# Context sums kept in memory between two cross attentions, and squares taken in one operation

## The chip, the cores and the metric

The kernel runs on one core of a Trainium2 chip. The metric is device time in microseconds (us) of one execution; a time given for a kernel is the median of several runs. The profile is of one further execution, with its own time.

The engines by the names of the profile: PE is the matrix engine (PEld its weight loads, which overlap the matmuls), DVE is VectorE, ACT is ScalarE, POOL is GpSimd, and SP is SyncE, which here only issues DMAs. A "q" behind a name is the engine's own instruction queue. Each engine takes its instructions in the order of its queue.

## The reference

Two layers are applied to `x` (8 x 64 x 512, float32) with a context of 8 x 1601 x 512. Each layer is a cross attention to the context, a self attention (the first layer's works on the Fourier transform of x), and a feed-forward part (a mixture of experts in layer 0, ternary weights in layer 1). What matters here are the two cross attentions, which read the same context:

```python
x = x + _L0_xattn_ref(_layernorm(x), ctx_1024, mask, L0_xattn_Wq, L0_xattn_Wkv, ...)
...
x = x + _L1_xattn_ref(_layernorm(x), ctx_1024, ctx_1024, L1_xattn_Wq, ..., L1_xattn_Wk, ..., L1_xattn_Wv, ...)
```

The first has 16 heads of 64; the kernel folds its key weights into the queries, so that scores are products of the context itself with folded queries, and mixes the context's rows before it applies the value weights. The second has 16 heads of 32, and projects keys and values of all 1601 tokens. Its keys and queries are normalized within each head (mean taken off, divided by the root of the mean square), so that it needs the sum of squares over each head of every key.

## The kernel before

**Seven products instead of eight.** The large products of both cross attentions are done by a scheme of Strassen and Winograd: both factors are cut into four quarters, and seven products of quarters or of sums of quarters replace eight. For the left factor (the context) the sums are made by POOL in `Quarters.left`, four operations at lines 136 to 139 on a tile `q` with seven slots. Slots 0 to 3 hold the loaded quarters, slots 4, 5 and 6 three of the sums, and the fourth sum overwrites slot 2:

```python
nc.gpsimd.tensor_add(q[:, 4, :], q[:, 2, :], q[:, 3, :])
nc.gpsimd.tensor_sub(q[:, 5, :], q[:, 4, :], q[:, 0, :])
nc.gpsimd.tensor_sub(q[:, 2, :], q[:, 0, :], q[:, 2, :])
nc.gpsimd.tensor_sub(q[:, 6, :], q[:, 1, :], q[:, 5, :])
```

**The first cross attention** (`l0_xattn`, from the start to about 1460 us) goes in 17 steps, two for each of the 8 batches (one for each half of the heads) and one behind. The first 12 x 128 tokens of a batch's context are six pairs of 128-token tiles. In each step `load_columns` (L177) loads the transposed context of the six pairs, two DMAs of 256 KB each (L183), and makes their sums with POOL operations of 128x256; the scores (matmuls at L465) use them. `load_rows` (L191, DMAs at L197) does the same with the rows of the context for `attend` (matmuls at L582). Columns and rows take turns in one pool of six buffers, so that a row pair can be loaded when the scores have used the column pair in its buffer, and the next column pairs when `attend` has used the rows. The transposed context of a batch is loaded twice, once for each half. Folded queries come by L224, value weights by L573, and the last 65 tokens by L651 and L662. The tail is not part of the quarters.

**The second cross attention** (`l1_xattn`, about 1840 to 3020 us) loads the transposed context once for each batch, as three groups of 512 tokens. `load` (L1426) has two DMAs of 512 KB for 256 tokens each (L1430), then `Quarters.left` with operations of 128x512: a quarter is 256 tokens by half of the 512 features. `project_keys` and `project_values` run the seven products with matmuls at L1514, through `Sevenfold`. A product is copied from the accumulator by ACT (`keep`, L1485), or added to a kept one by DVE (`sum`: L1493 for keys, L1506 for values), or finished by ACT (`last`, L1497 and L1509). During the attention of batch b the program projects the values of b and the keys of b + 1, and as soon as group g has given its values, `load(b + 1, g)` refills its buffer. The scores are matmuls at L1689 and are scaled by DVE at L1701. The softmax has DVE folds over key tiles (L1709 to L1714, for the maximum and the sum), a subtraction (L1731), and ACT's Exp (L1732). The weighted sum of values is L1740.

When the keys of two column groups of 128 features are done, `finish` (L1789) calls `squares_of` and `deviations` for each of the two. `squares_of` (L1548) squares the 1601 keys in four ACT operations of 384, 384, 384 and 449 elements (L1552) into four buffers, `deviations` sums each piece over heads with one matmul (L1564), copies the sums (L1566, L1567), turns them (L1570), and POOL raises them to the power -1/2 (L1577).

At its start, the second attention projects the last 65 tokens of all batches and stores them in memory (keys L1606, values L1617, copied from the accumulators by ACT at L1605 and L1616).

**What sets the order.** The program text does not set the order of an engine's queue. A planner in the compiler goes through the program with its own model of times and puts an instruction into its engine's queue when the model finds it ready, earlier program lines first among those ready. It also sets all waits. SP's queue is made in the same way, and an instruction in it that waits holds up those behind it.

Of the kernel before, what the change touches and what calls it, by code (L numbers as in the profile page):

```python
# [10 lines left out]
F32 = mybir.dt.float32  # L11
# [3 lines left out]
AF = mybir.ActivationFunctionType  # L15
# [5 lines left out]
P = 128  # L21
B, S, D = 8, 64, 512
NT = B * S // P
DC = D // P
NKV = 1601
# [94 lines left out]
QH = HALF // 2  # L120
NPAIR = LAST // 2
# [17 lines left out]
        nc.gpsimd.tensor_sub(q[:, 6, :], q[:, 1, :], q[:, 5, :])  # L139


def l0_xattn(K, x, d, ternary):

# [5 lines left out]
    tc, nc = K.tc, K.nc  # L149
    with ExitStack() as es:  # L150
        wp = es.enter_context(tc.tile_pool(name="a_w", bufs=1))
        cp = es.enter_context(tc.tile_pool(name="a_ctx", bufs=NPAIR))
# [21 lines left out]
            pool, tag = ((ps_x, "x"), (ps_y, "y"), (ps_z, "z"), (ps_m, "mm"))[turn[0] % 4]  # L174
            return pool.tile(shape, F32, tag=tag, name=name)

        def load_columns(b):  # L177

            pairs = []
            for i in range(NPAIR):  # L180
                q = cp.tile([P, 7, QH], F32, tag="pair", name="ctxT")
                for j in range(2):
                    nc.sync.dma_start(  # L183
                        q[:, ds(2 * j, 2), :].rearrange("p h (c n) -> p (h c) n", n=P),
                        d["ctxT"][b, :, ts(2 * i + j, P)].rearrange("(c p) n -> p c n", p=P),
                    )
                Quarters.left(nc, q)
                pairs.append(q)
            return pairs

# [114 lines left out]
        m32 = wp.tile([B * NK, P], F32, tag="m32", name="m32")  # L305
        nc.scalar.dma_start(m8, d["mask"])
        load_tails(0)
        ctxT = load_columns(0)
        place = [tp.tile([P, 4, 3, QH], F32, tag="pt", name="stage").rearrange("p a b q -> p (a b q)") for _ in range(2)]
        qk = wp.tile([P, DC, HALF], F32, tag="qk", name="qk")  # L310
        qT = piece([NG, P], "qT")
# [333 lines left out]
        for step in range(2 * B + 1):  # L645
            if step < 2 * B:
                b, half = divmod(step, 2)
                if step:
                    now, ctxT = queries_of(b, half), load_columns(b)
                    if half == 0:  # L650
                        nc.sync.dma_start(  # L651
                            ctxT_tail[:, :, :TAIL], d["ctxT"][b, :, LAST * P :].rearrange("(c p) n -> p c n", p=P)
                        )
                s, m = scores(b, now, ctxT)
                top = top_of(m)
                if step == 1:
                    between = keys_side_of_rest(columns_of(norm_rest, NT - 1))
            if before:
                b0, half0 = divmod(step - 1, 2)
                attend(half0, *before, load_rows(b0), o[:, :, b0 % 2, :], step == 1)  # L660
                if half0 and b0 + 1 < B:
                    nc.sync.dma_start(ctx_tail[:TAIL], d["ctx"][b0 + 1, LAST * P :, :])  # L662
# [732 lines left out]
        self.fourth()  # L1395


def l1_xattn(K, x, d, ahead, queries_done, in_last):

# [6 lines left out]
    with ExitStack() as es:  # L1406
# [1 line left out]
        ep = es.enter_context(tc.tile_pool(name="d_e", bufs=1, reuse_waits="tile"))  # L1408
        cp = es.enter_context(tc.tile_pool(name="d_c", bufs=GROUPS, reuse_waits="tile"))
        wp = es.enter_context(tc.tile_pool(name="d_w", bufs=1, reuse_waits="tile"))  # L1410
        qp = es.enter_context(tc.tile_pool(name="d_sq", bufs=4, reuse_waits="tile"))
        rp = es.enter_context(tc.tile_pool(name="d_r", bufs=2, reuse_waits="tile"))
        ps_x = es.enter_context(tc.tile_pool(name="d_ps_x", bufs=2, space=PSUM, reuse_waits="tile"))
        ps_y = es.enter_context(tc.tile_pool(name="d_ps_y", bufs=2, space=PSUM, reuse_waits="tile"))
# [10 lines left out]

        def load(b, g):  # L1426

            q = cp.tile([P, 7, 2 * SET], F32, tag="ctxT", name="ctxT")
            for j in range(2):
                nc.sync.dma_start(  # L1430
                    q[:, ds(2 * j, 2), :].rearrange("p h (c n) -> p (h c) n", n=SET),
                    d["ctxT"][b, :, ds((2 * g + j) * SET, SET)].rearrange("(c p) n -> p c n", p=P),
                )
            Quarters.left(nc, q)
            return q

        def rights(w, name):
# [40 lines left out]
        class Keys:  # L1478
# [7 lines left out]

            def to(self, i, j):
                c = self.m + 2 * j
                return kT[c][:, ds((2 * self.g + i) * SET, SET)], bk[:, c : c + 1]

            def sum(self, i, j, ps, other):
                out, bias = self.to(i, j)
                nc.vector.scalar_tensor_tensor(out, ps, bias, other, ALU.add, ALU.add)  # L1493

            def last(self, i, j, ps):
                out, bias = self.to(i, j)
                nc.scalar.activation(out, ps, AF.Identity, bias=bias, scale=1.0)  # L1497

        class Values(Keys):


            def to(self, i, j):
                return v[:, 4 * self.g + 2 * i + self.m, ts(j, QH)]

            def sum(self, i, j, ps, other):
                nc.vector.tensor_add(self.to(i, j), ps, other)  # L1506
# [13 lines left out]
        def project_keys(q, g, m):  # L1520
            run.add(
                product(
                    lambda n, e: wk_of[n][:, e, ts(m, P)],
                    lambda n, e: q[:, Quarters.LEFT[n], ts(e, SET)],
                ),
                Keys(g, m),
            )

        def project_values(q, g, i):
            run.add(  # L1530
                product(
                    lambda n, e: q[:, Quarters.LEFT[n], ds(e * SET + i * P, P)],
                    lambda n, e: wv_of[n][:, e, :],
                ),
                Values(g, i),
            )
# [718 lines left out]
def program(tc, d):  # L2255
    nc = tc.nc
    with tc.tile_pool(name="const", bufs=1) as cp, tc.tile_pool(name="memory", bufs=1, space=DRAM) as memory:
# [5 lines left out]
        l0_xattn(K, x, d, w)  # L2263
# [26 lines left out]
        with tc.tile_pool(name="early", bufs=NT - 1) as sp:  # L2290

            def in_last():
                known.extend(K.statistics(sp, x[:, t : t + 1, :]) for t in range(NT - 1))

            l1_xattn(K, x, d, ahead, queries.close, in_last)
            keys.close()
            l1_tail(K, x, d, w, known)

# [93 lines left out]
```

## Time and profile before

| | |
|---|---|
| runs | 3199.24 us median of 3 (3198.28 to 3200.02) |
| profiled execution | 3206.62 us |
| its span, first to last instruction | 3204.8 us |
| mean granted clock of PE in it | 0.972 |
| POOL in `Quarters.left`, first attention, columns: 4 x 96 operations of 128x256 | 302.8 us |
| the same, rows | 296.6 us |
| POOL in `Quarters.left`, second attention: 4 x 24 operations of 128x512 | 146.8 us |
| POOL at L1577: 32 operations | 277.1 us |
| ACT at L1552: 96 operations of 384 (516 ns) and 32 of 449 (571 ns) | 67.8 us |
| DMA, mean over the span | 109 GB/s |

How to read the profile: a line of the timeline gives the start and the duration in us, the engine, the line of the kernel, the operation, what it writes and reads, shapes, and how many instructions are merged; in brackets stands how long the engine had been idle before it, and who ended that. A line of the waits gives who waited for whom, the time in total, how many times, and the longest. A line of the windows gives for a stretch of time its length and the busy time of PE, PEld, DVE, ACT and POOL (with instruction counts), then the mean granted clock of PE as a share of full speed, the share of the DMA engines' time in use, and GB/s.

### The profile page before, as it was taken

The page shows a single profiled execution, that of the slowest core. Times are in us where ns is not written, and L with a number is a line of the kernel's source. Part 1 is how long each engine was busy: PE and PEld are TensorE (multiplying, and loading weights), DVE is VectorE, ACT ScalarE, POOL GpSimd, SP SyncE. Part 2 cuts the span into 40 slices and gives each one's busy share as a digit, 9 for nine tenths or more (in the row PEclk, how much of TensorE's full clock was granted, in tenths as well). Part 3 has the DMA queues.
Part 4 walks back from the last instruction along what each step waited for, and adds up shares of the span by engine and source line. Part 5 has one row for each costly group of instructions (what it writes and reads, how often), then busy time and mean ns, then how long its engine had stood idle before and what let it go on. Part 6 is the DMA issues. An engine that isn't in the chain of part 4 may idle for free.

```text
span 3204.8 us, 42460 instructions
## 1 busy us (share of the span) xinstructions
PE 3080.4 (96%) x16347; PEld 2319.3 (72%) x16353; DVE 1895.4 (59%) x3168; ACT 855.8 (27%) x1716; POOL 1132.7 (35%) x1052
## 2 busy tenths in 40 slices
PE   8999999999999999999999999999999999999886
PEld 7777778888887788886544466777777777777653
DVE  4745555565566666665332346775756657576646
ACT  2222232222122322221122232323233232323223
POOL 5433325455444444441100053334253333424000
PEclk9999999999999999999999999989999999999788
DMA  7354554233434543226599632010101101010250
GB/s 215 92 166 145 157 177 121 89 109 106 138 92 142 186 139 99 89 85 221 181 350 340 220 95 86 7 41 9 56 17 31 45 17 41 26 35 3 102 83 14
DMA packets 341495, 349.88 MB, mean 109 GB/s; under 512 B 41102, under 2 KB 255126, under 8 KB 340142
## 3 DMA queue, kind: packets, MB, share of 16 engines
q1 hardware_dynamic: 335065, 329.84, 33.3%
q10 hardware_dynamic: 5589, 15.24, 1.3%
q8 instruction: 130, 2.13, 0.3%
q0 software_dynamic: 640, 2.10, 0.2%
q14 instruction: 71, 0.58, 0.1%
HBM read 315.07 MB, written 32.05 MB: 108 GB/s over the span
## 4 chain that ended last, share of the span: by engine, by line
PE 54%; DVE 8%; ACT 2%; issue 2%; DMA 1%; POOL 0%; SPq 0%; POOLq 0%; ACTq 0%; DVEq 0%
PE x_ps L1514 9%; PE y_ps L1514 7%; PE s_ps L1689 4%; PE acc L1740 4%; PE oe_ps L1228 3%; PE h_ps L1201 3%; PE x_ps L582 3%; PE x_ps L465 3%; PE sum_ps L1564 2%; PE z_ps L582 2%; PE z_ps L465 1%; DVE s L1701 1%; DVE s L1731 1%; PE y_ps L582 1%; ACT s L1732 1%
## 5 line engine op out<-in xcount | busy, mean ns | idle before, releaser
L1577 POOL TENSOR_TENSOR r<-r,minus_half 128x52 f32<-128x52 f32 x32 | 277.1, 8675 | 353.7 <-DVE r L1576 353.7
L136 POOL TENSOR_TENSOR ctxT<-ctxT 128x256 f32<-128x256 f32 (+1 forms) x120 | 112.3, 936 | 659.0 <-DMA ctxT<-in_ctxT 449.6
L465 PE MATMUL x_ps<-qt,ctxT 128*128 128x256 f32 x1152 | 285.9, 382 | 7.2 <-DVE s L430 4.0
L582 PE MATMUL x_ps<-pt,ctx 128*128 128x256 f32 x1152 | 280.4, 381 | 4.0 <-DVE a L558 3.1
L465 PEld LDWEIGHTS x_ps<-qt,ctxT 128*128 128x128 f32 x1152 | 216.2, 190 | 49.2 <-DVE s L430 9.2
L582 PEld LDWEIGHTS x_ps<-pt,ctx 128*128 128x128 f32 x1152 | 216.3, 189 | 38.0 <-DVE a L558 3.2
L1689 PEld LDWEIGHTS s_ps<-qb,kT 64*128 64x128 f32 x1664 | 175.7, 208 | 63.1 <-issue 29.2
L1689 PE MATMUL s_ps<-qb,kT 64*128 64x128 f32 x1664 | 208.4, 314 | 9.7 <-DVE s L1701 8.4
L446 DVE TENSOR_TENSOR m<-m,s 128x512 f32<-128x512 f32 x176 | 140.4, 798 | 92.2 <-ACT s L444 89.5
L136 POOL TENSOR_TENSOR ctx<-ctx 128x256 f32<-128x256 f32 x96 | 72.3, 753 | 340.1 <-DMA ctx<-in_ctx 286.2
L1701 DVE TENSOR_TENSOR s<-s_ps,r 128x512 f32<-128x512 f32 x192 | 126.3, 681 | 33.8 <-PE s_ps L1689 31.4
L1740 PEld LDWEIGHTS acc<-s,v 128*64 128x64 f32 x1664 | 99.5, 141 | 51.9 <-issue 42.3
L498 DVE TENSOR_TENSOR s<-s,top_ps 128x1024 f32<-128x1024 f32 (+1 forms) x112 | 123.2, 1136 | 21.6 <-PE top_ps L488 21.6
L1731 DVE TENSOR_TENSOR s<-s,top_ps 128x1664 f32<-128x1664 f32 x64 | 117.9, 1884 | 30.3 <-PE top_ps L1727 30.3
L430 DVE SCALAR_TENSOR_TENSOR s<-y_ps,bias,p 128x256 f32<-128x256 f32 x96 | 46.3, 483 | 143.9 <-PE y_ps L465 143.6
L1740 PE MATMUL acc<-s,v 128*64 128x128 f32 x1664 | 125.2, 286 | 5.7 <-ACT s L1732 5.7
L1732 ACT ACTIVATE s<-s 128x1664 f32<-128x1664 f32 x64 | 101.7, 1591 | 73.9 <-DVE s L1731 73.9
L499 ACT ACTIVATE s<-s 128x1024 f32<-128x1024 f32 (+1 forms) x112 | 110.8, 996 | 26.9 <-DVE s L498 22.6
L1514 PE MATMUL x_ps<-wv_of,ctxT 128*128 128x256 f32 x384 | 100.3, 395 | 18.3 <-DVE v L1506 18.3
L1201 PE MATMUL h_ps<-w,tok 128*128 128x512 f32 x256 | 117.3, 593 | 0.0
L1228 PE MATMUL oe_ps<-w,hT 128*128 128x512 f32 x256 | 115.6, 593 | 0.0
L139 POOL TENSOR_TENSOR ctxT<-ctxT 128x256 f32<-128x256 f32 (+1 forms) x120 | 115.6, 963 | 0.0
(471 smaller groups left out, 6542.3 us busy)
## 6 DMA issues: line engine op xcount, KB each, us to landing
w<-in_L0f_W SPq DMA_DIRECT2D x64, 1024.0 KB
ctxT<-in_ctxT SPq DMA_DIRECT2D x192, 256.0 KB
ctx<-in_ctx SPq DMA_DIRECT2D x192, 256.0 KB
ctxT<-in_ctxT SPq DMA_DIRECT2D x48, 512.0 KB
wvT<-in_L0x_WvT SPq DMA_DIRECT2D x16, 1024.0 KB
qk<-qk_all SPq DMA_DIRECT2D x15, 1024.0 KB
qk_all<-stage SPq DMA_DIRECT2D x32, 384.0 KB
wraw<-in_L1f_w1T SPq DMA_DIRECT2D x16, 512.0 KB
```

The costliest lines, as they stand in the source:

```text
L136: nc.gpsimd.tensor_add(q[:, 4, :], q[:, 2, :], q[:, 3, :])
L446: nc.vector.tensor_max(self.m, self.m if k else self.s[:, LAST, :], self.s[:, k, :])
L465: nc.tensor.matmul(ps, lhsT=ctxT[i][:, Quarters.LEFT[n], ts(e, P)], rhs=right[n][:, e, :], start=start and e == 0, stop=e == 1, skip_group ...
L582: nc.tensor.matmul(ps, lhsT=ctx[pair][:, Quarters.LEFT[n], ts(m, P)], rhs=right[n][:, i, :], start=start and i == 0, stop=i == 2, skip_gro ...
L1201: nc.tensor.matmul(ps, lhsT=self.tok[:, c, :], rhs=self.w1[n][:, c, :], start=c == 0, stop=c == DC - 1)
L1228: nc.tensor.matmul(ps, lhsT=self.hT[:, f, :], rhs=self.w2[f // 4][:, f % 4, :], start=f == 0, stop=f == 15)
L1514: nc.tensor.matmul(ps, lhsT=left(n, e), rhs=right(n, e), start=start and e == 0, stop=e == 1, skip_group_check=not start,)
L1577: nc.gpsimd.tensor_tensor(r, r, minus_half, ALU.pow)
L1689: nc.tensor.matmul(pair[j][:, i, :], lhsT=kT[c][rows, ts(k0 + i, P)], rhs=qb[rows, c, :], start=True, stop=True,)
L1701: nc.vector.tensor_mul(out, in_, by)
L1731: nc.vector.tensor_sub(s[:, j], s[:, j], ps[:, j, :].unsqueeze(1).to_broadcast([P, NK, P]))
L1740: nc.tensor.matmul(acc[ds(64 * j, 64), c, :], lhsT=v[:, k, ds(c * P + 64 * j, 64)], rhs=s[:, j, k, :], start=k == 0, stop=k == NK - 1,)
```

## The change

The first attention gets eight DRAM tiles `kept`, one for each batch, 128 x 6 x 4 x 256 float32 (3 MB each). In the first of a batch's two steps, `load_columns` stores the four sums of every pair there, with two DMAs on SP behind the POOL operations. The second step of a batch makes its sums as before and stores nothing.

The second attention no longer calls `Quarters.left`. A group is now two of the pairs of the first attention, in the same layout: a quarter is 128 tokens by half of the features, and the group's tile has a place for each of the two pairs. For each pair, `load` reads from the context the first tile whole (256 KB) and of the second the half that is used as it is (128 KB), and from `kept` the sums (128 KB and 384 KB): eight DMAs for a group. The products take their left or moving factor across both pairs, and keys and values are written to the places where the new order of tokens puts them: keys in two pieces of 128 columns.

`squares_of` squares the 1601 keys of a column group in one operation into one buffer (before: four buffers, each as long as the longest piece); the four sums in `deviations` read their parts of it.

```diff
-        def load_columns(b):
+        def load_columns(b, keep=False):
...
                 Quarters.left(nc, q)
+                if keep:
+                    nc.sync.dma_start(kept[b][:, i, 3, :], q[:, 2, :])
+                    nc.sync.dma_start(kept[b][:, i, 0:3, :], q[:, 4:7, :])
                 pairs.append(q)
...
-        ctxT = load_columns(0)
+        ctxT = load_columns(0, True)
...
-                    now, ctxT = queries_of(b, half), load_columns(b)
+                    now, ctxT = queries_of(b, half), load_columns(b, half == 0)
...
-        qp = es.enter_context(tc.tile_pool(name="d_sq", bufs=4, reuse_waits="tile"))
+        qp = es.enter_context(tc.tile_pool(name="d_sq", bufs=1, reuse_waits="tile"))
...
-            q = cp.tile([P, 7, 2 * SET], F32, tag="ctxT", name="ctxT")
-            for j in range(2):
+            q = cp.tile([P, 2, 7, QH], F32, tag="ctxT", name="ctxT")
+            for u in range(2):
+                i = 2 * g + u
                 nc.sync.dma_start(
-                    q[:, ds(2 * j, 2), :].rearrange("p h (c n) -> p (h c) n", n=SET),
-                    d["ctxT"][b, :, ds((2 * g + j) * SET, SET)].rearrange("(c p) n -> p c n", p=P),
+                    q[:, u, 0:2, :].rearrange("p h (c n) -> p (h c) n", n=P),
+                    d["ctxT"][b, :, ts(2 * i, P)].rearrange("(c p) n -> p c n", p=P),
                 )
-            Quarters.left(nc, q)
+                nc.sync.dma_start(
+                    q[:, u, 3, :].rearrange("p (c n) -> p c n", n=P),
+                    d["ctxT"][b, SET:, ts(2 * i + 1, P)].rearrange("(c p) n -> p c n", p=P),
+                )
+                nc.sync.dma_start(q[:, u, 2, :], kept[b][:, i, 3, :])
+                nc.sync.dma_start(q[:, u, 4:7, :], kept[b][:, i, 0:3, :])
...
-                return kT[c][:, ds((2 * self.g + i) * SET, SET)], bk[:, c : c + 1]
+                of = kT[c][:, ds(2 * self.g * SET, 2 * SET)].rearrange("p (u i n) -> p i u n", i=2, n=P)
+                return of[:, i], bk[:, c : c + 1]
...
-                return v[:, 4 * self.g + 2 * i + self.m, ts(j, QH)]
+                return v[:, 4 * self.g + 2 * self.m + i, ts(j, QH)]
...
-                    lambda n, e: q[:, Quarters.LEFT[n], ts(e, SET)],
+                    lambda n, e: q[:, :, Quarters.LEFT[n], ts(e, P)],
...
-                    lambda n, e: q[:, Quarters.LEFT[n], ds(e * SET + i * P, P)],
+                    lambda n, e: q[:, i, Quarters.LEFT[n], ts(e, P)],
...
-            made = []
-            for k0, n in CK:
-                sq = qp.tile([P, CK[-1][1]], F32, tag="sq", name="sq")
-                nc.scalar.activation(sq[:, :n], kT[c][:, ds(k0, n)], AF.Square)
-                made.append(sq)
-            pending.append((made, r))
+            sq = qp.tile([P, NKV], F32, tag="sq", name="sq")
+            nc.scalar.activation(sq, kT[c][:, :NKV], AF.Square)
+            pending.append((sq, r))
...
-                for (_, n), i in zip(CK, range(4)):
-                    nc.tensor.matmul(ps[ds(32 * i, 32), :n], lhsT=sel, rhs=squares[i][:, :n], start=True, stop=True)
+                for i, (k0, n) in enumerate(CK):
+                    nc.tensor.matmul(ps[ds(32 * i, 32), :n], lhsT=sel, rhs=squares[:, ds(k0, n)], start=True, stop=True)
...
+        kept = [memory.tile([P, NPAIR, 4, QH], F32, tag=f"kept{b}", name="kept") for b in range(B)]
```

More of the change, by code (lines that the diff above doesn't have):

```diff
@@ L139, in left, with l0_xattn @@
         nc.gpsimd.tensor_sub(q[:, 6, :], q[:, 1, :], q[:, 5, :])
-def l0_xattn(K, x, d, ternary):
+def l0_xattn(K, x, d, ternary, kept):
     tc, nc = K.tc, K.nc
@@ L1395, in end, with l1_xattn @@
         self.fourth()
-def l1_xattn(K, x, d, ahead, queries_done, in_last):
+def l1_xattn(K, x, d, ahead, queries_done, in_last, kept):
     tc, nc = K.tc, K.nc
@@ L1488, in to @@
                 c = self.m + 2 * j
-                return kT[c][:, ds((2 * self.g + i) * SET, SET)], bk[:, c : c + 1]
+                of = kT[c][:, ds(2 * self.g * SET, 2 * SET)].rearrange("p (u i n) -> p i u n", i=2, n=P)
+                return of[:, i], bk[:, c : c + 1]
             def sum(self, i, j, ps, other):
                 out, bias = self.to(i, j)
+                ps, other = (a.rearrange("p (u n) -> p u n", n=P) for a in (ps, other))
                 nc.vector.scalar_tensor_tensor(out, ps, bias, other, ALU.add, ALU.add)
@@ L1496, in last @@
                 out, bias = self.to(i, j)
-                nc.scalar.activation(out, ps, AF.Identity, bias=bias, scale=1.0)
+                nc.scalar.activation(
+                    out, ps.rearrange("p (u n) -> p u n", n=P), AF.Identity, bias=bias, scale=1.0
+                )
         class Values(Keys):
             def to(self, i, j):
-                return v[:, 4 * self.g + 2 * i + self.m, ts(j, QH)]
+                return v[:, 4 * self.g + 2 * self.m + i, ts(j, QH)]
             def sum(self, i, j, ps, other):
@@ L2262, in program @@
         slots, done = (memory.tile([CAP * E_, D], F32, tag=n, name=n) for n in ("slots", "done"))
-        l0_xattn(K, x, d, w)
+        kept = [memory.tile([P, NPAIR, 4, QH], F32, tag=f"kept{b}", name="kept") for b in range(B)]
+        l0_xattn(K, x, d, w, kept)
         with tc.tile_pool(name="experts", bufs=4) as ep, tc.tile_pool(name="gate", bufs=1, reuse_waits="tile") as gp:
@@ L2293, in in_last @@
                 known.extend(K.statistics(sp, x[:, t : t + 1, :]) for t in range(NT - 1))
-            l1_xattn(K, x, d, ahead, queries.close, in_last)
+            l1_xattn(K, x, d, ahead, queries.close, in_last, kept)
             keys.close()
```

## The prediction

> **What bounds the kernel now.** I read the page first, then the waits of PE in the second cross attention, then the timeline around the longest of them, then the windows for the clock.
>
> ```profile
> span 3204.8 us, 42460 instructions
> PE 3080.4 (96%) x16347; PEld 2319.3 (72%) x16353; DVE 1895.4 (59%) x3168; ACT 855.8 (27%) x1716; POOL 1132.7 (35%) x1052
> ```
>
> PE is busy 96% of the span, so a change that touches only POOL, ACT and DMA can gain only where PE waits for what they delay. The waits of PE between 1880 and 2960 us, the second cross attention behind its start:
>
> ```profile
> PE x_ps L1514 <- DVE v L1506: 17.8, 6, 3.7
> PE s_ps L1689 <- DVE s L1701: 8.0, 23, 1.1
> PE qT_ps L1659 <- DVE q L1345: 6.4, 2, 3.8
> ```
>
> Six stalls of the projections, one for each of batches 1 to 6, and two of the queries in batch 0: always VectorE is late. The timeline at the second of the six tells why:
>
> ```profile
> 2273.53 2.04 DVE L1709 TENSOR_TENSOR fold<-s 128x768 f32<-128x768 f32 x1 [0.66 <-ACT s L1732]
> ...
> 2274.71 1.99 POOL L138 TENSOR_TENSOR ctxT<-ctxT 128x512 f32<-128x512 f32 x1
> ...
> 2275.83 1.69 DVE L1710 TENSOR_TENSOR fold<-fold,s 128x768 f32<-128x768 f32 x1
> ...
> 2276.66 1.98 POOL L139 TENSOR_TENSOR ctxT<-ctxT 128x512 f32<-128x512 f32 x1
> ...
> 2277.55 1.90 DVE L1711 TENSOR_TENSOR fold<-fold,s 128x768 f32<-128x768 f32 x1
> ...
> 2280.17 0.42 DVE L1506 TENSOR_TENSOR v<-y_ps,u 128x256 f32<-128x256 f32 x1
> ...
> 2281.31 2.07 PE L1514 MATMUL x_ps<-wv_of,ctxT 128*128 128x256 f32 x4 [2.82 <-DVE v L1506]
> ```
>
> While POOL makes the sums of a loaded group (L136 to L139), the folds take 2.04, 1.69 and 1.90 us. Undisturbed they take about 0.95:
>
> ```profile
> L1711 DVE TENSOR_TENSOR fold<-fold,s x59: 940/948/1908, 1994.8 to 2954.9; 128x768 f32<-128x768 f32 x59
> ```
>
> (min/median/max in ns.) The growth is 1.09 + 0.74 + 0.96 = 2.79 us, and PE behind them waits 2.82. I read the same off the timeline at all nine long stalls with those sums beside them: in batch 0 3.74 and 2.63 us of waiting against 3.57 and 2.40 of growth (small scaling operations, L64 to L69, some at 1.2 us instead of 0.17), at 2106.8 1.06 against 1.00, and the six 2.82, 2.82, 2.78, 3.69, 2.93, 2.76 against 2.39, 2.79, 2.36, 3.68, 2.51, 2.73. Together 25.2 us of waiting, 23.4 of growth.
>
> Each is followed by a slow stretch: the four matmuls at 2281.31 take 2.07 us, elsewhere 1.03. The windows (PEclk is the third column from the end):
>
> ```profile
> 2281.00:2291.50 10.50, 10.19 (x47) 8.71 (x48) 5.33 (x9) 0.37 (x1) 1.50 (x2) 0.51 0.34 102
> ...
> 2260.00:2400.00 140.00, 135.38 (x854) 106.23 (x853) 93.61 (x152) 41.29 (x82) 54.26 (x17) 0.96 0.09 27
> ```
>
> Some 10 us at half clock after a stall, and a mean of 0.96 over a batch of 140 us. Over 1880 to 2960, (1 - clock) x length by such windows is 40 us lost.
>
> **The change, part by part.**
>
> *Sums read instead of made (second attention).* It removes 24 x 4 POOL operations of 128x512, 147 us by the POOL rows, none on PE's path itself. It takes away what they do to VectorE: **-23 us** of waiting (the growth, not the whole 25). The clock: gaps of 0.84 and 0.85 us at 2389.1 and 2668.0 were not followed by half clock, and what remains of the nine is below 0.5 us each. So I count 7/8 of the 40: **-35 us**. What is late next is the 8.0 us of L1689 waiting for L1701, in pieces of at most 1.1; it stays.
>
> [...]
>
> *Loads of the second attention.* A group is 8 DMAs of 1792 KB in all instead of 2 of 1024 KB. In the steady batches: the two loads of a group are issued at 2266.5, its sums end at 2278.6 and its keys are projected from about 2295. Issue at 0.45 us each and the longer transfer (5.6 us for 1 MB by the rows at 2099.5 to 2105.2) give 8 to 10 us, less than the 12.1 now. Cost 0; cover 17 us. At the start it is different. Three groups are loaded at 1853 to 1864, and behind them in SP's queue stand the stores of the value tails (L1617 at 1864.2). ACT's copy L1616 waits 10.5 us for these until 1870.7, the copy of a product (L1485) stands behind it at 1874.26, and PE waits 2.3 us for it. The 2.4 MB more take 7 us at 342 GB/s (the fastest window, 1600 to 1760). From 0 (stores planned earlier) to 10 (7 of waiting and 3 of clock); I take **+7**, since the copy waits through the whole transfer today.
>
> *Stores in the first attention.* Eight batches, 6 pairs, two stores each on SP: 96 issues, 25 MB. Each waits for POOL's last sum of its pair, and later loads may stand behind it. The order is a planner's, not the program's: in the step at 640 us a load of the step before (L662) went out between those of pair 0 and the rest.
>
> ```profile
> 639.55 0.93 SPq L183 DMA_DIRECT2D ctxT<-in_ctxT  x2
> 640.81 0.34 SPq L662 DMA_DIRECT2D ctx_tail<-in_ctx  x1
> 641.25 17.15 SPq L183 DMA_DIRECT2D ctxT<-in_ctxT  x10
> ```
>
> So the stores of pairs 0 to 2 should stand at 647 to 653, while SP waits for buffers anyway (pair 3 is issued at 655.1), and those of 3 to 5 at 663 to 669, before the first row load at 670.5. The columns of pair 3 are ready at 662.8 and used from about 680; the third pair of rows is ready at 689.6 and used at 697.0. A store of 512 KB takes 1.5 us at 342 GB/s. Cost 0, cover 7 us (rows) and 17 (columns). A pair's buffer now also waits for its store, which ends over 10 us before PE releases it. In step 0 the DMA engines are 73% busy (0 to 80 us), and 3.1 MB are 9 us of them: 0 to 9, I take **+2**, for PE there waits for VectorE and ACT.
>
> *One Square.* 96 operations at 516 ns and 32 at 571 become 32; by the row of Exp over 1664 elements (1591 ns) I estimate 1.54 us each: ACT does 68 us now, then 49, and gains PE nothing. But the first sum (L1564) now waits for the whole group and its last key, then four sums follow at 0.33 us: about 1.5 us later, 32 times, and with one buffer the next Square waits for them. Today attention products (L1740) stand between the sums and hide this. From -7 (PEld's whole wait for sq, 6.6 us, goes) to +48 (cover gone everywhere); I take **+3**, nearest to the covered rows at 2179 to 2190.
>
> *Layout.* The keys are written in two pieces of 128 instead of 256 in a row. A split copy of 384 elements (L50) takes 554 ns and a 512 one 691: no price for the split. 0.
>
> **Sum.** -23 - 35 + 7 + 2 + 3 = -46. The profiled execution is 3206.6 us (span 3204.8 and 1.8 around it), so 3160.6; it stands 7.4 above the median of the runs, 3199.2, so I predict **3153**.
>
> **Rivals.**
> 1. *The clock falls anyway.* The plan is made anew, and another short wait at the same place (six more stalls of L1701, now hidden) keeps the half-clock stretches. Only the waiting goes: -23 + 12 = -11, **3188**. For it: the folds and L1506 stay in one queue. Against: growth and wait agree within 0.5 us nine times.
> 2. *Half of the fall.* In batch 0 the stretches at 1953.4 and 1980.7 are 3.5 us long (clock 0.51 in those windows), 1.7 lost in each. If that is a stall's own share everywhere and the rest of the 40 has another cause, 9 x 1.7 = 15 goes: -23 - 15 + 12 = -26, **3173**. Against it: the 10 us stretches, too, begin right behind the stalls, and none begins elsewhere in those batches. [...]
> 3. *The Square is on the path.* Its whole 48 us instead of 3: **3198**, no change. For it: two finishes a batch, POOL's 8.7 us power behind each. Against: sums lie among other matmuls now.
> 4. *Slower: stores hold up the loads on SP.* If each pair's stores stand before the next pair's loads, a pair takes 3.5 (landing) + 2.9 (sums) + 1.8 (issues) = 8.2 us; the sixth pair of columns is ready near 687, just in time for 692, and the third pair of rows near 701.5 instead of 689.6. It decides once the rows are over 7.4 us late: then PE waits 4.5 us and loses some 5 to the clock, in seven steps 67: 3153 + 67 = **3220**. Against it is the order shown above.
> 5. *It does not do what it says* I leave out: the loads of the second attention no longer call the POOL sums.
>
> **How the numbers follow.** Forecast 0.50, with its own range 3130 to 3176; rival 1 0.18, rival 2 0.05, rival 3 0.10, rival 4 0.17. A measurement of this kernel tells about 0.2% (6.4 us) from no change. Faster: 0.50 + 0.18 + 0.05 = 0.73; same 0.10; slower 0.17. The range leaves out rival 4. Its low end has all of 25 + 40, the start's stall gone too (4) and the sums' wait gone (7): 3206.6 - 76 - 7.4, about 3125; its high end is rival 3 with the 7 us that step 0 may cost beyond my 2: 3205.
>
> **What would show it.** Right: folds at no more than 1.0 us between 1880 and 2960, no wait of L1514 for L1506 above 1 us, clock 0.99 or more in windows of 140 us, POOL without 128x512 sums after 1850. Wrong: PEclk still 0.96 there (rival 1); PE waiting for sq, or sums no longer among other matmuls (3); PE waits for POOL ctx in the first attention (4); a gap above 5 us near 1872 means that the start costs more than I took.

## The result and the profile after

The changed kernel takes 3126.33 us (median of 4 runs, 3113.29 to 3132.08). Its ratio to the kernel before is 0.9757, with a 95% interval from 0.9718 to 0.9796: 2.4% faster, about 78 us (73 by the two medians, 3199.63 and 3126.33). A second comparison, beside the experiments, gave 0.9731 (0.9704 to 0.9757). The prediction was 3153 us, a gain of 46: the direction was right, the gain was about 30 us too small. By its median the result stands just inside the low end of the range (3125 us), by its ratio just below it (0.9757 of 3199.24 is 3121.5).

The page of the changed kernel, span and busy time:

```profile
span 3124.9 us, 42614 instructions
PE 3008.4 (96%) x16353; PEld 2284.7 (73%) x16353; DVE 1852.9 (59%) x3168; ACT 846.8 (27%) x1620; POOL 992.6 (32%) x956
```

PE is still busy 96% of the span, but it is busy 72 us less with the same matmuls (16353 and 16347 records). A saving of waits would have left the busy time as it was; half clock explains part of it, and the rest is the first sign of what the prediction missed.

The waits of PE in the second attention (1880 to 2960 us; L1699 was L1689, L1711 was L1701, L1527 was L1514, L1519 was L1506):

```profile
PE s_ps L1699 <- DVE s L1711: 6.8, 27, 0.5
...
PE x_ps L1527 <- DVE v L1519: 1.8, 4, 0.5
```

The six stalls of 2.8 to 3.7 us are gone, and the small waits for the scaled scores stay as before. The fold that took up to 1908 ns (min/median/max, same view as before), and the window of one batch:

```profile
L1721 DVE TENSOR_TENSOR fold<-fold,s x64: 941/950/959, 2004.3 to 2935.6; 128x768 f32<-128x768 f32 x64
```

```profile
2260.00:2400.00 140.00, 137.85 (x933) 110.96 (x932) 97.46 (x168) 41.65 (x74) 34.54 (x4) 1.00 0.19 58
```

None of these folds takes over 0.96 us, POOL has 4 operations left of 17 in such a window, and the clock is 1.00 instead of 0.96. So far all is as forecast. To see the rest I cut both profiles at the same three places (first matmul of the rest of layer 0, first matmul of the second attention, first transpose behind its last weighted sum). In each part "waits" are the gaps over 0.2 us in which neither a matmul nor a weight load runs, "clock" is half of the time at half clock, and "rest" is what is left of the length:

| us, before / after | length | waits | clock | rest |
|---|---|---|---|---|
| first attention | 1498.5 / 1521.7 | 30.6 / 44.5 | 3.4 / 15.4 | 1464.5 / 1461.9 |
| between | 338.3 / 337.7 | 5.9 / 5.3 | 5.1 / 5.1 | 327.2 / 327.3 |
| second attention | 1181.6 / 1079.6 | 47.2 / 24.7 | 54.6 / 8.5 | 1079.7 / 1046.4 |
| end | 186.4 / 185.9 | 31.6 / 31.2 | 25.6 / 23.9 | 129.2 / 130.8 |

Two rows don't fit the forecast. The second attention loses 102 us instead of 48, and 33 of these are neither waits nor clock. And the first attention grows by 23 us instead of 2.

**The 33 us.** Grouping PE's matmuls by line, and counting for each the time to the start of the next, shows one line that changed by more than some 4 us: the sums of squares over heads. Before (timeline of a steady batch; a sum is two matmul records):

```profile
2183.50 0.94 PE L1564 MATMUL sum_ps<-sq,c_heads 128*32 128x449 f32 x2
...
2185.21 1.41 ACT L1552 ACTIVATE sq<-kT 128x384 f32<-128x384 f32 x3
...
2185.67 1.36 PE L1564 MATMUL sum_ps<-sq,c_heads 128*32 128x384 f32 x6
...
2186.20 0.14 PEld L1564 LDWEIGHTS sum_ps<-sq,c_heads 128*32 128x32 f32 x2 [0.28 <-ACT sq L1552]
...
2187.54 0.94 PE L1564 MATMUL sum_ps<-sq,c_heads 128*32 128x449 f32 x2
```

After:

```profile
2176.09 0.96 PE L1574 MATMUL sum_ps<-sq,c_heads 128*32 128x384 f32 x8
```

One sum alone takes as long as four together. Each of the four sums of a column group has 32 output columns, and the four go to four different blocks of 32 output partitions. In the raw starts of the last row, the four first matmuls begin 7 ns apart. Over the whole second attention, by how many sums stand next to each other in PE's queue:

| sums together | 1 | 2 | 3 | 4 | PE time in all |
|---|---|---|---|---|---|
| before: groups, mean us | 40, 0.84 | 8, 0.77 | 20, 1.22 | 3, 0.91 | 66.9 us |
| after | 0 | 0 | 0 | 32, 0.91 | 29.1 us |

With four Squares each sum was ready at its own time, and the planner put other matmuls between them. With one Square all four are ready at once and run side by side. That is 38 us, of which part is not PE's own time but a wait that no gap shows, because by the profile the matmuls before it still run: in each of the 20 groups of three the last sum starts some 50 ns after its Square has ended (in the group at 2185.67 its Square ends at 0.48 us and it starts at 0.53). By 20 x (1.22 - 0.84) I estimate this part at 8 us and PE's own at 30. The rest of the second attention shrank by 33 and not 38, since other lines grew by some 5 in all.

So sums that stand together cost PE little more than one: four took 0.91 us here, where four alone would take 4 x 0.84 = 3.36 us, a factor of 3.7.

**The 23 us.** New waits of PE in the first attention (0 to 1520 us), and the wait of SP in front of the new stores:

```profile
PE x_ps L468 <- ACT u L428: 7.6, 5, 5.2
...
PE x_ps L585 <- DVE a L561: 5.4, 1, 5.4
```

```profile
SPq L189 <- POOL ctxT L138: 97.2, 46, 3.4
```

SP stood 97 us waiting for POOL with a store at the head of its queue, 46 times. The timeline at one of the new stalls shows who waited behind it (all engines):

```profile
1102.26 0.32 SPq L190 DMA_DIRECT2D kept<-ctxT  x1
1102.67 0.38 SPq L1908 DMA_DIRECT2D w_out<-wq  x1
1105.32 1.15 ACT L1906 ACTIVATE wq<-wraw,wdown 128x1024 bf16<-128x1024 f32 x1 [16.84 <-DMA w_out<-wq]
1106.49 0.38 SPq L1882 DMA_DIRECT2D wraw<-in_L1f_w2T  x1
1106.50 0.43 DVE L1907 TENSOR_SCALAR wq<-wq 128x1024 bf16<-128x1024 bf16 x1 [6.15 <-ACT wq L1906]
1106.84 0.42 DVE L561 TENSOR_TENSOR a<-x_ps,p 128x256 f32<-128x256 f32 x1
...
1107.32 0.79 PE L585 MATMUL x_ps<-pt,ctx 128*128 128x256 f32 x1 [5.44 <-DVE a L561]
```

Not the context loads are late, but a chain that has nothing to do with the attention: the rounding of layer 1's ternary weights, which the planner wove into these steps. The store of one rounded weight (L1908) stands behind six stores of sums. Its buffer comes free late, ACT rounds the next weight late (L1906), VectorE has the next step of that weight (L1907) in its queue ahead of L561, and PE waits 5.4 us for L561. At the same place before, PE waited 3.1 us. At 1128 us the same chain holds ACT itself: L1906, which waits 5.8 us for a store of a rounded weight, stands ahead of the L428 that PE waits 5.2 us for.

### The profile page after: what moved, and what is told of

Read it like the earlier page. It is cut to its first block, busy times and chain, and to the rows that moved or that the text cites. A ratio compares the mean times of both kernels' runs of the same rounds, so it can differ in the third digit from the quotient of the medians.

```text
span 3124.9 us, 42614 instructions
## 1 busy us (share of the span) xinstructions
PE 3008.4 (96%) x16353; PEld 2284.7 (73%) x16353; DVE 1852.9 (59%) x3168; ACT 846.8 (27%) x1620; POOL 992.6 (32%) x956
## 4 chain that ended last, share of the span: by engine, by line
PE 52%; DVE 6%; ACT 3%; issue 1%; DMA 1%; POOL 0%; POOLq 0%; ACTq 0%; DVEq 0%
PE x_ps L1527 9%; PE y_ps L1527 7%; PE acc L1750 4%; PE oe_ps L1231 4%; PE h_ps L1204 4%; PE s_ps L1699 3%; PE x_ps L585 3%; PE x_ps L468 2%; PE z_ps L585 2%; PE z_ps L468 1%; DVE s L1711 1%; PE sum_ps L1574 1%; ACT s L1742 1%; DVE s L1741 1%; PE y_ps L585 1%
## 5 line engine op out<-in xcount | busy, mean ns | idle before, releaser
L136 POOL TENSOR_TENSOR ctxT<-ctxT 128x256 f32<-128x256 f32 x96 | 81.1, 845 | 419.3 <-DMA ctxT<-in_ctxT 253.6
L1699 PEld LDWEIGHTS s_ps<-qb,kT 64*128 64x128 f32 x1664 | 156.3, 189 | 56.3 <-issue 24.3
L1699 PE MATMUL s_ps<-qb,kT 64*128 64x128 f32 x1664 | 186.5, 291 | 9.6 <-DVE s L1711 6.8
L1711 DVE TENSOR_TENSOR s<-s_ps,r 128x512 f32<-128x512 f32 x192 | 126.7, 683 | 21.0 <-PE s_ps L1699 20.3
L501 DVE TENSOR_TENSOR s<-s,top_ps 128x1024 f32<-128x1024 f32 (+1 forms) x112 | 123.5, 1140 | 23.9 <-PE top_ps L491 23.9
L1750 PE MATMUL acc<-s,v 128*64 128x128 f32 x1664 | 117.8, 281 | 5.7 <-ACT s L1742 5.7
L515 DVE TENSOR_TENSOR total<-total,s 128x512 f32<-128x512 f32 x160 | 110.2, 689 | 3.5
L468 PE MATMUL x_ps<-qk,ctxT 128*128 128x256 f32 x384 | 105.3, 392 | 7.0 <-ACT s L447 4.2
```

The costliest lines, as they stand in the source:

```text
L468: nc.tensor.matmul(ps, lhsT=ctxT[i][:, Quarters.LEFT[n], ts(e, P)], rhs=right[n][:, e, :], start=start and e == 0, stop=e == 1, skip_group ...
L1699: nc.tensor.matmul(pair[j][:, i, :], lhsT=kT[c][rows, ts(k0 + i, P)], rhs=qb[rows, c, :], start=True, stop=True,)
L1711: nc.vector.tensor_mul(out, in_, by)
L1750: nc.tensor.matmul(acc[ds(64 * j, 64), c, :], lhsT=v[:, k, ds(c * P + 64 * j, 64)], rhs=s[:, j, k, :], start=k == 0, stop=k == NK - 1,)
```

## The experiments

All ratios are to the kernel before, measured beside each kernel; intervals are 95%.

### One Square alone, four Squares alone, stores alone, no stores

Four kernels take the change apart. The first is the kernel before with only the edit of the Squares.

```diff
-            for k0, n in CK:
-                sq = qp.tile([P, CK[-1][1]], F32, tag="sq", name="sq")
-                nc.scalar.activation(sq[:, :n], kT[c][:, ds(k0, n)], AF.Square)
+            sq = qp.tile([P, NKV], F32, tag="sq", name="sq")
+            nc.scalar.activation(sq, kT[c][:, :NKV], AF.Square)
```

> The kernel before with the single Square of 1601 keys and its one buffer as its only edit; context sums are still made by POOL in both attentions and nothing is stored. Theory A (read from the two traces): the four sums of a column group, which go to four different 32-column parts of PE, are ready at the same moment and run beside one another, 0.9 us for four instead of 2.1, so 32 x 1.2 = 38 us go: about 3161 us, and the half-clock stretches of the second attention stay (clock about 0.97). Theory B (the prediction's term): the sums wait for the Square, +3: about 3202 us. Rival 3 of the prediction (the Square on the path): +48, 3247 us.

Measured: 3166.67 us, ratio 0.9888 (0.9843 to 0.9933), a gain of 36 us. Theory A holds, and the prediction's +3 and its rival 3 (+48) fall.

The second is the changed kernel with that edit taken back.

> The changed kernel with the four Squares and four buffers of the kernel before; sums still stored and read back. Theory A (sums side by side are worth 38 us): about 3164 us, with a pitch of about 0.26 us from one of these sums to the next instruction of PE instead of 0.11. Theory B (the Square costs 3): about 3123 us.

Measured: 3165.69 us, ratio 0.9881 (0.9837 to 0.9924). Against 0.9757 with one Square that is 40 us (48 against 0.9731), from the other side. Its sums stand in 71 groups again and take 69.8 us of PE.

The third is the kernel before with the stores alone.

```diff
                 Quarters.left(nc, q)
+                if keep:
+                    nc.sync.dma_start(kept[b][:, i, 3, :], q[:, 2, :])
+                    nc.sync.dma_start(kept[b][:, i, 0:3, :], q[:, 4:7, :])
```

> The kernel before with the 96 stores of the first attention as its only edit; the second attention makes its sums on POOL as before and reads nothing back. Theory A (the stores hold up other transfers in SP's queue): the first attention grows by the 23 us that it grew in the changed kernel, about 3222 us, with stalls of PE at the same places (near 92, 1100 and 1130 us). Theory B (the prediction): +2, about 3201 us. Theory C (the 23 us are an accident of the new order, which any edit of the plan can bring): somewhere between 3195 and 3230, with stalls at other places.

Measured: 3216.69 us, ratio 1.0039 (1.0018 to 1.0061), 12 us slower (6 to 20). In its profile the first attention takes 1515.6 us and has stalls of 4.1, 4.8 and 5.6 us at 90, 1096 and 1121 us, the places of the changed kernel. Theory A is right on the mechanism and the places. Its 23 us was one profile's figure and twice what the runs show.

The fourth is the changed kernel without stores.

```diff
-                if keep:
-                    nc.sync.dma_start(kept[b][:, i, 3, :], q[:, 2, :])
-                    nc.sync.dma_start(kept[b][:, i, 0:3, :], q[:, 4:7, :])
...
-        kept = [memory.tile([P, NPAIR, 4, QH], F32, tag=f"kept{b}", name="kept") for b in range(B)]
+        kept = [
+            d["ctx"][b, : P * NPAIR * 2, :].rearrange("(p r) n -> p (r n)", p=P).rearrange(
+                "p (i s q) -> p i s q", i=NPAIR, s=4
+            )
+            for b in range(B)
+        ]
```

> The changed kernel without the 96 stores; the second attention reads the same number of bytes in the same shapes from rows of the context in place of the kept sums, so its keys and values are not the reference's. Theory A: the first attention falls back to its length before, 23 us less than in the changed kernel: about 3103 us. Theory B (stores cost 2): about 3124 us. Theory C (accident of the order): between 3095 and 3130.

Measured: 3111.62 us, ratio 0.9714 (0.9659 to 0.9768). That is 5 to 14 us below the changed kernel (0.9731 and 0.9757), and the intervals overlap; its first attention takes 1501.5 us, without the two stalls of about 5 us behind 1090.

Together with before and after these make a table with pairs of rows that differ in one thing:

| us in the profile | sums by POOL | stores | Squares | first attention | second: waits | second: clock | second: rest |
|---|---|---|---|---|---|---|---|
| before | yes | no | 4 | 1498.5 | 47.2 | 54.6 | 1079.7 |
| one Square alone | yes | no | 1 | 1503.7 | 47.8 | 37.5 | 1046.0 |
| stores alone | yes | yes | 4 | 1515.6 | 48.1 | 42.7 | 1082.1 |
| four Squares | no | yes | 4 | 1513.6 | 24.9 | 6.8 | 1089.2 |
| no stores | no | no | 1 | 1501.5 | 24.9 | 6.8 | 1046.2 |
| after | no | yes | 1 | 1521.7 | 24.7 | 8.5 | 1046.4 |

Each column follows one cause: the waits and the clock of the second attention follow POOL's sums, its rest follows the Squares, and the first attention follows the stores. One number fits less well: with four Squares the rest is 7 to 10 us longer where the sums are read (1089.2) than where they are made. The effect of reading the sums instead of making them is the difference of two rows: 0.9881 - 1.0039 with four Squares (51 us), 0.9714 - 0.9888 with one (56 us). Waits, clock and rest added, the table gives 52 and 53.

### Two Squares

> The changed kernel with two Squares (768 and 833 keys, two buffers) in place of one; everything else as changed. Theory A (PE pays some 0.87 us for each group of sums that stands together in its queue, whether it holds one sum or four): 2 groups for each column group instead of 1, 32 x 0.87 = 28 us more than the changed kernel, about 3154 us. Theory B (what counts is ACT's time, 68 us of Squares before and 49 changed, some 55 here): at most 6 us more, about 3130 us.

Measured: 3140.74 us, ratio 0.979 (0.975 to 0.9831), 11 to 19 us more than the changed kernel: between the theories. The profile says why. The sums stand in 53 groups, not 64, since 17 times both Squares were done before the first sum was placed; they take 46.1 us of PE, 17 more than in the changed kernel. So the price per group is right (46.1 / 53 = 0.87), and my count of groups was wrong. Theory B (ACT's time) asked for 6 at most and is the worse account.

### Work for POOL put back

```diff
+            for u in range(2):
+                for n in range(4):
+                    nc.gpsimd.tensor_add(spare, q[:, u, n, :], q[:, u, 4, :])
             return q
```

> The changed kernel with work for POOL put back into the second attention: for each loaded group eight additions of 128x256 whose result nobody reads, about as long as the four of 128x512 of the kernel before. Nothing waits for them but the release of the group's buffer. Theory A (POOL beside VectorE stretches VectorE, PE waits and the clock falls): PE's waits in the second attention go from 25 us back to about 48 and its loss to the clock from 8 to 35 or 45, so 3126 + 23 + 27 to 37 = 3176 to 3186 us. Theory B (the gain came with the new layout, loads and order of the second attention): within 10 us of the changed kernel, about 3130 us.

Measured: 3151.65 us, ratio 0.9839 (0.9794 to 0.9884), 26 to 35 us more than the changed kernel (0.9757 and 0.9731). PE's waits of L1514's kind in the second attention (the last number is the longest):

```profile
PE x_ps L1532 <- DVE v L1524: 12.8, 7, 2.4
```

So POOL beside VectorE brings stalls back by itself, without being on the path of the data; theory B falls. But it brings about half: 26 to 35 us by the runs instead of 50 to 60; in the profile waits of 36.3 instead of 48, and 17.1 of clock instead of 35 to 45 (the profiled run was the fastest of the four, with the highest clock). The stalls are 1.8 to 2.4 us long here and were 2.8 to 3.7, and only two of the six were followed by half clock. VectorE was stretched less: its folds grew by 25 us in all over their undisturbed times, against 34 in the kernel before, and none of them took over 1.5 us, against 2.04. Why the stretch is smaller with additions of 256 instead of 512 elements was not followed up, so 16 to 30 of the 51 to 56 us are not shown to be POOL beside VectorE.

### The stores: which queue, how many, in which step

The next kernels ask what of the stores costs the first attention its time. Issued by POOL, behind its own sums:

```diff
-                    nc.sync.dma_start(kept[b][:, i, 3, :], q[:, 2, :])
-                    nc.sync.dma_start(kept[b][:, i, 0:3, :], q[:, 4:7, :])
+                    nc.gpsimd.dma_start(kept[b][:, i, 3, :], q[:, 2, :])
+                    nc.gpsimd.dma_start(kept[b][:, i, 0:3, :], q[:, 4:7, :])
```

> The changed kernel with the 96 stores issued by POOL itself, behind its sums, instead of SP. Theory A (the stores cost by holding SP, where they wait for POOL, with loads and the ternary weights' transfers behind them): the first attention falls from about 1520 us to about 1502, the stalls near 1100 and 1125 us go, 3105 to 3113 us in all. Theory B (the 25 MB written beside the loads cost it): about 3126 us, stalls as they are. Theory C (POOL's issues delay its next sums so far that PE waits for them): above 3135 us.

Measured: 3113.09 us, ratio 0.9707 (0.9664 to 0.9749). The stalls near 1100 and 1125 fell to 3.1 us and below 1; but a stall of 4.6 us appeared at 400, and the first attention takes 1511.2 us in the profile, not 1502. The time is at the upper end of theory A, and theories B and C fall; but the first attention came only half of the way from 1520 to A's 1502.

One store for each pair, five slots instead of four:

```diff
+                    nc.sync.dma_start(kept[b][:, i], q[:, 2:7, :])
...
+                nc.sync.dma_start(q[:, u, 2:7, :], kept[b][:, i])
```

> The changed kernel with one store for each pair instead of two, of slots 2 to 6 (the four sums and the quarter between them, 640 KB instead of 512), and two loads for each pair in the second attention instead of four (the same bytes). 48 issues fewer on SP in the first attention, 96 fewer in the second; the store waits for POOL's last sum. Theory A (SP is held by the wait for POOL, not by the number of issues): the stalls near 1100 and 1125 us stay, 3120 to 3128 us. Theory B (the number of issues counts): half of the stores' cost goes, 3113 to 3120 us.

Measured: 3117.52 us, ratio 0.972 (0.968 to 0.976). The stalls stay (4.5 us at 1099, 3.3 at 1127), as theory A says, but shorter; the time lies between the two.

Both edits together, and both with the stores in the second of a batch's two steps (`load_columns(b, half == 1)`), with the changed kernel beside them:

> The changed kernel with both edits together: one store of slots 2 to 6 for each pair, issued by POOL. Theory A (SP held by the waits for POOL is the larger part, POOL's own issues of about 1 us each the rest, both now halved or gone): the first attention at about 1505 us instead of 1511 with either edit alone, no stall above 3 us near 1100 or 1125, and 3105 to 3110 us by median. Theory B (what is left is the 31 MB themselves on the DMA engines): 1511 us, about 3113 us.

> As the run before it, with the stores moved to the second of a batch's two steps, so that none stands in the first step, where the DMA engines are busiest. Theory A (the first step's transfers compete): the stalls near 70 and 91 us fall back to 1.0 and 2.2 us and the half clock behind them with it, 3 to 7 us less than the run before it, about 3102 us. Theory B (no competition there once SP is free): no difference above 3 us.

> The changed kernel itself, beside the two others of this call on the same chip. Expected as measured at first: about 3126 us, ratio to before 0.976, between 0.972 and 0.980, the first attention at 1514 to 1522 us.

Measured: 3124.47 us, ratio 0.9747 (0.9719 to 0.9775); 3115.27 us, 0.972 (0.9694 to 0.9746); and the changed kernel 3120.28 us, 0.9731 (0.9704 to 0.9757). First attentions in the profiles 1510.9, 1507.3 and 1516.1 us. The first of the three is no gain over the changed kernel, against my expectation (its issues by POOL take 0.54 and 0.57 us in the trace of the kernel with two stores by POOL, not 1), and the differences are within the intervals: inconclusive.

Two stores by POOL, in the second step:

> The changed kernel with its two stores for each pair issued by POOL, in the second of a batch's two steps; loads of the second attention as changed. Theory A (the stores' cost is SP's wait for POOL and the first step's transfers, both avoided here): the first attention at 1503 to 1508 us against 1514 to 1522 changed, ratio to before 0.969 to 0.972, about 3108 us. Theory B (what the stores cost beyond that comes from POOL's own issues, twice as many as with one store): 1511 us and more, ratio 0.972 to 0.975.

Measured: 3108.76 us, ratio 0.9706 (0.9681 to 0.9732). The first attention takes 1501.6 us, as without stores. Last, the same step with SP's queue:

> The changed kernel with its two stores for each pair still issued by SP, but in the second of a batch's two steps. It completes a table of queue and step: SP and first step 1514 to 1522 us of first attention, POOL and first step 1511, POOL and second step 1502. Theory A (the queue is what costs: SP waits for POOL in whichever step): 1512 to 1520 us, stalls above 4 us again among the ternary weights' transfers (1000 to 1200 us), ratio to before about 0.975. Theory B (the step is what costs): 1502 to 1506 us, ratio about 0.971.

Measured: 3127.49 us, ratio 0.9756 (0.9726 to 0.9786), first attention 1521.9 us: theory A. The stalls near 1100 us are short now (1.9), and another one takes their place. SP's timeline in the first step of this kernel:

```profile
66.74 0.34 SPq L189 DMA_DIRECT2D kept<-ctxT  x1
...
75.37 0.34 SPq L190 DMA_DIRECT2D kept<-ctxT  x1
75.80 1.01 SPq L183 DMA_DIRECT2D ctxT<-in_ctxT  x2
76.91 0.56 SPq L227 DMA_DIRECT2D qk<-qk_all  x1
```

```profile
PE x_ps L468 <- DMA qk<-qk_all: 13.0, 1, 13.0
```

The load of the folded queries (L227) is issued at 76.9 behind stores that wait for POOL, and PE waits 13 us for it. With POOL as the issuer and the same step the same load goes out at 65.7, and PE has no such wait. So with the stores in this step it is the queue: a transfer behind them is late, and which one it is changes with the plan. In the first step the queue decides less: 1511.2 us by POOL against 1511.4 to 1521.7 by SP. Why POOL's stores cost some 10 us there in the profile is open, and the runs (0.9707 and 0.9706) don't show it. The time of the issues alone I estimate at 96 x 0.32 = 31 us of SP (0.32 us is the median of L189 and of L190 in the changed kernel), which only issues, so PE would lose nothing by it. The measurement shows more: in the second step the queue is worth 20 us of the first attention (1521.9 by SP, 1501.6 by POOL, same bytes) and 16 us by the ratios, since an issue that waits holds up those behind it, here L227 until 76.9 instead of 65.7.

Of the kernels that keep the sums, the one with two stores by POOL in the second step has the lowest ratio, not apart from three others (0.9707, and 0.972 twice). It beats the kernel before by 2.9%. Against the changed kernel (0.9757 and 0.9731) the runs alone don't separate it; the profile of the first attention does (1501.6 against 1511.4 to 1521.7 in seven profiles with stores by SP in the first step).

## Why the prediction was wrong

By its own steps:

- **Sums read instead of made, -23 and -35: right.** Waits in the second attention went from 47.2 to 24.7 us, which is -22.5. The clock's loss went from 54.6 to 8.5 in the two profiles, and from 37.5 to 54.6 down to 6.8 to 8.5 in the six of the table. The prediction's 40 is the part of it between 1880 and 2960: there 39.3 became nothing (taken from 43 us behind the start of the second attention to 58 before its end). The 8.5 that stayed lie at its end, by a wait of 5.2 us that both kernels have. The two pairs of kernels measure -51 and -56 for this part, against -58 forecast. Rivals 1 (the clock falls anyway) and 2 (half of the fall) are out.
- **One Square, +3: this step failed.** It is -36 from the side of before and -40 to -48 from the side of after. I priced the edit by when its results are ready, let the four sums follow one another at 0.33 us, and looked for PE waiting. I did not ask what the sums cost PE itself, though the timeline of before had rows of one sum in 0.94 us and of three in 1.36 beside each other. In its place the runs showed sums that run side by side when they are ready together: 71 groups in 66.9 us became 32 groups in 29.1, and two Squares gave 53 groups in 46.1. My bound of -7 to +48 was therefore a bound on waits alone. The sums do wait for the Square (PEld 9.5 us for ACT, before 6.6), as forecast, but that is the small term. The sign that the prediction set for rival 3, sums no longer among other matmuls, came true, and it was the gain.
- **Stores in the first attention, +2: mis-sized.** They cost 12 us (6 to 20) from the side of before, 5 to 14 from the side of after. Rival 4 had the right mechanism, SP held by stores that wait for POOL, and the wrong victim: I followed the loads of columns and rows, whose cover of 7 and 17 us was enough. Behind the stores stood the ternary weights' transfers too, which I had not followed because they belong to another part of the program. The price was a fifth of the rival's 67, as it struck at three or four places, not in seven steps.
- **Start of the second attention, +7: wrong, 0.** The planner put the copies of the products ahead of the value tails' copies (L1626) on ACT, so that PE no longer waits there; the stall of 2.3 us at 1872 went too, as the profile after has no gap above 0.8 us in that place. The prediction named that case as its lower bound and took the other.
- **Steady loads and layout, 0: right with one Square.** The rest of the second attention is 1046.0 with the old layout and 1046.4 with the new one. With four Squares it is 7 to 10 us longer in the new one; 3 of these are at the sums (69.8 against 66.9), where the third waits longer for its Square, and the others are spread over other lines and stay open.

Along one chain of kernels the terms add up by construction: +12 for the stores, -51 for the sums and -40 for the Square are, but for rounding, the -78 of the ratio 0.9757. What the experiments add is that each term has about the same size in another order: -56 for the sums, -36 for the Square. Each of these is uncertain by 7 to 23 us, as I estimate from the intervals; the waits, the clock and the rest of the profiles agree with them more closely.

That the time came near the low end of the range is partly luck. That end was made of waits and clock alone and left no room for a gain in PE's own time, and the stores, 10 us dearer than forecast, hid a part of the Square's gain.

Of the 23 us by which the profiled first attention grew, only part is the stores' usual price: six profiles with SP's stores in the first step as changed, or with an edit elsewhere, have 1513.6 to 1521.7 us (mean 1516.2), three without stores 1498.5 to 1503.7 (mean 1501.2). The profiled execution was the worst of these.

## What to carry to other kernels

An edit that makes several results ready at the same moment can change what stands next to what in the next engine's queue: look whether those neighbours can share the engine (here four sums in 0.91 us, one in 0.84) before pricing the edit by its wait. When a queued instruction is given a wait, follow every transfer behind it in that queue to whoever needs it, those of other parts of the program first, since they are the ones that nobody covers (here L1908, and PE waited 5.4 us). And put a store on the queue of the engine that makes its data, where it need not wait for another engine, if that engine has the time (here 1501.6 us of first attention by POOL and 1521.9 by SP, with the stores in the second step).

## What the runs showed of the hardware

- **Sums side by side.** One sum of 384 or 449 columns takes PE 0.84 us on average, two together 0.77, four 0.91; the first matmuls of four begin 7 ns apart. Three took 1.22 to 1.37, more than four, because the last of them waited for its Square in every such group.
- **When the clock falls.** In 15 profiles of this study, between 1885 and 2900 us, 23 gaps of PE were over 2.5 us long, and 21 of them were followed by half clock within some 5 us; of 38 gaps from 1.0 to 2.5 us, 6 were. The stretches at half clock last 3.4, 6.8, 10.2 or 13.7 us, half of them 10.2.
- **The scatter is the clock.** The four runs of the kernel with POOL's work put back go from 3134.34 us at a granted clock of 0.984 to 3161.0 at 0.976; 0.008 of 3150 us is 25 us, nearly the whole difference. The second attention's loss to the clock is 54.6, 37.5 and 42.7 us in the profiles of the three kernels whose POOL makes its sums. So a term that is read from one profile's clock should carry some 10 us of doubt, an estimate from these three.
- **VectorE beside POOL.** The folds of 128x768 take up to 2.0 us beside POOL's sums and 0.95 otherwise. The scaling of the scores, which reads PE's accumulators, takes at most 0.69 us beside them and otherwise. Beside POOL's power (L1577, 8.7 us) the folds take 0.96 us at most, as undisturbed.
